# Nineteen filler products added in the first chunk, and three small sums moved from GpSimd to VectorE

## The chip, the cores and the metric

The kernel runs on one core of a Trainium2 chip. The core has five engines with a queue each: TensorE (PE in the profile, with its weight loads as PEld), VectorE (DVE), ScalarE (ACT), GpSimd (POOL) and SyncE (SP), which here only starts DMA transfers. An engine takes its instructions strictly in the order in which they were written into its queue, and waits on semaphores for what other engines must have done. The metric is the device time of one execution in microseconds, as the median of several runs.

## The reference

The input x has 2 sequences of 1024 steps and 128 channels. Four residual layers follow one another, each on a normalised x:

```python
x = x + attn_a(layernorm(x))   # projections, a scan with a decay per channel, norm, projection
x = x + ffn(layernorm(x))      # 8 experts: silu(x @ w_gate) * (x @ w_up) @ w_down, weighted
x = x + attn_b(layernorm(x))   # small MLPs, a recurrence with an 8x8 state per head, norm, MLP
x = x + ffn(layernorm(x))      # the same experts again
```

Each norm takes the mean and the variance of 128 channels and multiplies by 1/sqrt(variance + eps). The weights of the experts (the gate) are a product of two softmaxes over 8 logits.

## The kernel before

The 1024 steps of both sequences are cut into five chunks, four of 192 steps and one of 256, so that a chunk has 384 or 512 columns. Each chunk passes through the layers in pieces named by a letter and the chunk's number: A (attention a), f and F (gate and experts of the first ffn), B, P, R, C, O, E (attention b), g and G (second ffn). The pieces of different chunks are interleaved; the products of the experts are the bulk of TensorE's work, and the rest is put between them.

What is written is not the final order. Every operation is recorded as a step, and the method `order` (L488) plays the steps through a model of the five engines: it gives each step a rank, a cost and a due time, and at each point hands the engine that is free the ready step of the lowest rank. Tiles get their places (buffers) in the same pass, and a step that wants a place waits till one is free. `emit` (L690) then writes the steps in that order, all from line L703, which is why nearly every line of the profile reads L703 and is told apart by its tiles. A change of one step's engine changes the planner's due times, and so can reorder the steps round it.

The planner also sets *fillers*: products of a tile called turn with itself (128x128, in one pass), whose result nobody reads. Where its model sees TensorE idle for more than FILL = 350 ns ahead of a step (L657), it computes a number of fillers from the gap, and `emit` writes them ahead of that step (L700). They go into a bank of PSUM that is free, or into the bank of the step itself.

The start of the program, which the change touches, runs as follows for chunk 0:

- `part_a` (L1063): norm a0, its transpose pt_a0, three projections, the scan, then the output's transpose pt_ao0, norm aon0 and the update of x.
- `gating` (L1125) for f0: norm f0, three transposes into the tile pt_f0, then xT_hi (ScalarE) and xT_lo (VectorE), the logits pl_f0 (nine small products with wr), two softmaxes, and the transposes pc_f0 of the weights.
- `fold_small` (L926), independent of x: three products into the tile pf, which ScalarE copies into the tile fold (Z_at in the profile); VectorE fills in the rest of fold; then seven small products of fold with columns of vec into the tile pb (`m_at<-vec_at,Z_at`), from which VectorE makes the tile bias.
- `experts` (L1181) for f0. In this first use of each expert's weights, ScalarE and VectorE cut them into two parts (`wgu_at<-Z_at`) in a ring of six places; later chunks reload the cut weights. A part of an expert takes six products (`g_at<-xT_hi_at,wgu_at` and `xT_lo_at`), a Silu on ScalarE into the tile h, and a multiplication on VectorE. The products go into four banks named g; a bank comes free when its Silu or its multiplication has read it.

The norms are made by `layernorm` (L969). For a0, aon0 and f0, VectorE makes mean and variance (bn_stats, bn_aggr), and these two lines follow:

```python
either(f"ve_{name}", "P").tensor_scalar(ve[:, 0 : k.nt], mv[:, 0 : k.nt, 1], eps, None, ALU.add)
...
nc.gpsimd.tensor_tensor(rs[:, 0 : k.nt], ve[:, 0 : k.nt], expo.to_broadcast([P, k.nt]), ALU.pow)
```

`either` picks the usual engine ("P", GpSimd) unless the site's name stands in the set ENG (L110), in which case it picks the other.

## Time and profile before

| what | value |
|---|---|
| median of 3 runs | 766.05 us (765.82 to 766.85) |
| the profiled execution's own time | 766.12 us |
| its span, first to last instruction | 764.3 us |
| TensorE busy | 734.7 us (96%) |
| VectorE busy | 605.1 us (79%) |
| ScalarE busy | 457.7 us (60%) |
| GpSimd busy | 430.3 us (56%) |
| mean granted clock of TensorE | 0.99 |

The profiled execution lies 0.07 us above the median, and 1.82 us of its time lie outside its span. A busy TensorE in such a profile is one with products in flight, since the ends of products are modelled. The granted clock is the share of full speed that TensorE was given; before the first event of a trace the profile shows 1.00 for want of a record. Times in the text are microseconds from the span's start.

### The profile page before, as it was taken

Reading aid. Unit: us, or ns where it says so; the run is one execution under the profiler, and the core shown is the slowest. Engines: PE = TensorE matmul, PEld = TensorE weight load, DVE = VectorE, ACT = ScalarE, POOL = GpSimd, SP = SyncE. Lnnn points to the kernel's source line nnn. Section 1 sums busy time; section 2 is a strip of 40 time slices with the busy share of each in tenths; the row PEclk is TensorE's granted clock in tenths of the full one; section 3 lists DMA queues with packets and bytes.
Section 4 is the critical chain, followed back from the end, with each engine's and each line's share of the span. In section 5 each row is a group of like instructions: output and inputs, shape, how many; then the busy total and the mean of one; then the engine's idle time right before and its main releaser. Section 6 shows DMA issues by size and latency. Waiting matters only on the chain.

```text
span 764.3 us, 12089 instructions
## 1 busy us (share of the span) xinstructions
PE 734.7 (96%) x3406; PEld 575.2 (75%) x3406; DVE 605.1 (79%) x1387; ACT 457.7 (60%) x913; POOL 430.3 (56%) x491
## 2 busy tenths in 40 slices
PE   7899999999989999999998998999999999999997
PEld 7888787887777877766667767787787777776664
DVE  6576644699989998999999999999999778344332
ACT  3665577649774775644897969655654553554332
POOL 3132322977445597656975599975975247530222
PEclk9799999999999999999999999999999999999999
DMA  7597568666866589866495693686667857746551
GB/s 232 163 297 247 158 179 218 218 199 201 207 214 205 169 210 285 230 177 177 122 260 142 180 298 111 191 271 195 198 203 246 237 150 222 236 135 192 177 165 42
DMA packets 131561, 152.14 MB, mean 199 GB/s; under 512 B 52950, under 2 KB 74518, under 8 KB 131494
## 3 DMA queue, kind: packets, MB, share of 16 engines
q1 hardware_dynamic: 130694, 150.88, 67.2%
q8 instruction: 28, 0.46, 0.2%
q10 hardware_dynamic: 800, 0.48, 0.2%
q14 instruction: 39, 0.32, 0.1%
HBM read 131.79 MB, written 19.53 MB: 198 GB/s over the span
## 4 chain that ended last, share of the span: by engine, by line
PE 58%; DVE 17%; ACT 8%; POOL 6%; issue 5%; DMA 5%; SPq 0%; DVEq 0%; POOLq 0%; ACTq 0%
PE g_at L703 49%; PE m_at L703 8%; DVE h_at L703 3%; ACT L703 3%; DVE bu_at L703 2%; POOL ox_at L703 2%; ACT h_at L703 1%; DVE Z_at L703 1%; DVE pz_at L703 1%; DVE q_at L703 1%; DVE ot_at L703 1%; POOL pm_at L703 1%; DMA d_v<-b_at 1%; DVE y_at L703 1%; ACT Zt_at L703 1%
## 5 line engine op out<-in xcount | busy, mean ns | idle before, releaser
L703 PE MATMUL g_at<-xT_hi_at,wgu_at 128*128 128x384 f32 (+1 forms) x1280 | 481.1, 416 | 11.0 <-DVE h_at L703 4.3
L703 PEld LDWEIGHTS g_at<-xT_hi_at,wgu_at 128*128 128x128 f32 x1280 | 239.3, 190 | 76.0 <-issue 12.9
L703 ACT ACTIVATE h_at<-g_at 128x384 f32<-128x384 f32 (+1 forms) x320 | 162.6, 512 | 189.1 <-PE g_at L703 180.5
L703 PE MATMUL g_at<-h_at,wd_at 128*128 128x384 f32 (+1 forms) x640 | 267.2, 509 | 2.3 <-POOL h_at L703 0.9
L703 DVE TENSOR_TENSOR h_at<-h_at,g_at 128x384 f32<-128x384 f32 (+1 forms) x302 | 172.6, 575 | 100.7 <-PE g_at L703 55.4
L703 PE MATMUL g_at<-xT_lo_at,wgu_at 128*128 128x384 f32 (+1 forms) x640 | 226.3, 354 | 0.0
L703 PEld LDWEIGHTS g_at<-xT_lo_at,wgu_at 128*128 128x128 f32 x640 | 121.8, 190 | 38.8 <-issue 12.5
L703 PEld LDWEIGHTS g_at<-h_at,wd_at 128*128 128x128 f32 x640 | 116.2, 189 | 22.8 <-issue 3.1
L703 POOL TENSOR_TENSOR de_at<-de_at,cb_at 128x384 f32<-128x384 f32 (+1 forms) x50 | 54.2, 1085 | 94.9 <-ACT de_at L703 94.9
L703 ACT ACT_TABLE_LOAD x64 | 82.1, 1283 | 5.1 <-DMA x_at<-in_x 4.0
L703 POOL TENSOR_TENSOR ds_at<-ds_at,de_at 128x384 f32<-128x384 f32 (+1 forms) x58 | 66.4, 1145 | 24.4 <-DVE de_at L703 22.5
L703 POOL TENSOR_TENSOR Z_at<-Z_at,vr_at 128x192 f32<-128x192 f32 (+1 forms) x75 | 49.4, 659 | 33.2 <-DVE Z_at L703 30.1
L703 DVE TENSOR_TENSOR q_at<-bu_at,kt_at 128x384 f32<-128x384 f32 (+1 forms) x75 | 43.8, 583 | 0.7
L703 ACT COPY Zt_at<-Z_at 128x384 f32<-128x384 f32 (+1 forms) x40 | 39.2, 984 | 7.8 <-DVE Z_at L703 5.9
L703 DVE TENSOR_REDUCE bu_at<-pz_at 128x48 f32<-128x384 f32 (+1 forms) x75 | 43.3, 578 | 0.6
L703 POOL TENSOR_TENSOR ox_at<-Zt_at,y_at 128x384 f32<-128x384 f32 (+1 forms) x36 | 41.0, 1153 | 4.7 <-DVE y_at L703 4.6
L703 DVE TENSOR_TENSOR Z_at<-Z_at,q_at 128x384 f32<-128x384 f32 (+1 forms) x75 | 42.9, 572 | 0.8
L703 DVE TENSOR_TENSOR pz_at<-Z_at,bu_at 128x384 f32<-128x384 f32 (+1 forms) x75 | 42.8, 570 | 0.4
L703 ACT COPY de_at<-g_at 128x384 f32<-128x384 f32 (+1 forms) x50 | 24.9, 499 | 29.0 <-PE g_at L703 26.4
L703 POOL TENSOR_TENSOR vr_at<-vt_at,rks_at 128x384 f32<-128x384 f32 (+3 forms) x40 | 35.7, 895 | 1.1
L703 POOL TENSOR_TENSOR om_at<-Z_at,rst_at 128x384 f32<-128x384 f32 (+1 forms) x25 | 32.1, 1283 | 3.4 <-DVE Z_at L703 3.4
L703 POOL TENSOR_TENSOR h_at<-h_at,h_at 128x384 f32<-128x384 f32 x18 | 18.3, 1019 | 18.0 <-ACT h_at L703 18.0
(228 smaller groups left out, 1021.6 us busy)
## 6 DMA issues: line engine op xcount, KB each, us to landing
wgu_at<-wcut SPq DMA_DIRECT2D x288, 256.0 KB, 3.0
wd_at<-in_w_down SPq DMA_DIRECT2D x80, 256.0 KB, 2.9
wcut<-wgu_at SPq DMA_DIRECT2D x32, 256.0 KB, 4.4
cb_at<-cd_f SPq DMA_DIRECT2D x32, 192.0 KB, 3.7
cb_at<-cd_g SPq DMA_DIRECT2D x32, 192.0 KB, 3.4
Z_at<-in_w_gate SPq DMA_DIRECT2D x8, 256.0 KB, 3.5
Z_at<-in_w_up SPq DMA_DIRECT2D x8, 256.0 KB
cb_at<-cd_f SPq DMA_DIRECT2D x8, 256.0 KB
```

The costliest lines, as they stand in the source:

```text
L703: getattr(engine, s.call)(*[placed(v) for v in s.args], **{n: placed(v) for n, v in s.kw.items()})
```

## The change

A table MORE names two tiles, pb with 12 and pt_f0 with 7. Ahead of the first step on TensorE that writes into one of them, so many fillers are written, into that tile's own bank; the planner's computed fillers apply to all other steps. The three names ve_a0, ve_aon0 and ve_f0 are added to ENG, so that the sum of variance and eps of these three norms is made by VectorE; the power that follows stays on GpSimd.

```diff
+MORE = dict(pb=12, pt_f0=7)
 FILL_FROM, FILL_TO, FILL = 3300.0, 1e9, 350.0
...
-    ol3_3 ol3_7 ol4_1 ol4_3 ol4_7 ot0_2 ot1_2 ot2_2 ot3_2 rr1 v00 v01 v02 v03 v04 v21 vb1 vc1 ve_g4 vt1
-    xb2 ym0_0 ym1_0 ym2_0 ym3_0 ym4_0 ym4_2 ym4_3
+    ol3_3 ol3_7 ol4_1 ol4_3 ol4_7 ot0_2 ot1_2 ot2_2 ot3_2 rr1 v00 v01 v02 v03 v04 v21 vb1 vc1 ve_a0
+    ve_aon0 ve_f0 ve_g4 vt1 xb2 ym0_0 ym1_0 ym2_0 ym3_0 ym4_0 ym4_2 ym4_3
...
-                if e == "T" and t > free[e] + FILL and t < FILL_TO:
-                    to = s.args[0].tile
+                to = s.args[0].tile if e == "T" else None
+                if e == "T" and to.name in MORE and all(o is s or o.start is None for o in to.users):
+                    s.turns = (MORE[to.name], to.ring, to.place)
+                elif e == "T" and t > free[e] + FILL and t < FILL_TO:
```

The built programs differ in their order as follows. Up to the products into pf the queues of TensorE are the same, with 16 instead of 17 fillers ahead of pf. Then:

- before: 2 products into pb, 3 transposes pt_f0, 3 pb, 4 products of f0's first two parts with xT_hi, 1 pb, 9 logits, the 8 other products of these parts, 1 pb, 5 fillers, 3 transposes pc_f0, the third part's products.
- after: 7 fillers, 3 transposes pt_f0, 12 fillers, 2 pb, 2 products with xT_hi, 9 logits, the 10 other products, 3 pb, 3 transposes pc_f0, 2 pb, the third part's products. The 5 fillers ahead of pc_f0 are gone.

On VectorE, the copies into fold now follow the normalisation of f0, and the cut wb_lo stands inside the softmax, between its second and third operation. On ScalarE, the casts of wgu_f0_1_2 and wgu_f0_1_3 now stand between the softmax's exponentials and the load of the Silu table, ahead of the first Silu, h_f0_0_0; before, they stood behind the third and the fourth Silu. On SP's queue, the write-backs of these two cuts and the transfer of the gate weights (cd_f0) now stand ahead of the second half of the fourth expert's load. All of this lies at the start: the last step that has another place in the order is number 122 of 2811 on TensorE, 121 of 1387 on VectorE, 75 of 811 on ScalarE, 23 of 484 on GpSimd and 60 of 708 on SP. Behind these the queues are the same in both programs.

## The prediction

> **What bounds the kernel now.** I read the page first (busy shares, the slices with the clock, the chain), then the stretches of the first 45 us, then the instructions there.

> ```profile
> span 764.3 us, 12089 instructions
> PE 734.7 (96%) x3406; PEld 575.2 (75%) x3406; DVE 605.1 (79%) x1387; ACT 457.7 (60%) x913; POOL 430.3 (56%) x491
> PEclk9799999999999999999999999999999999999999
> PE 58%; DVE 17%; ACT 8%; POOL 6%; issue 5%; DMA 5%; SPq 0%; DVEq 0%; POOLq 0%; ACTq 0%
> ```

> TensorE is busy for 96% and carries 58% of the chain that ended last. Its clock is below full in one early slice, the second. All queues are the same in both programs behind TensorE's step 122 (the products pya_1, at about 43 us), so what the change is worth is how much earlier or later the engines stand there; TensorE is then busy without a gap (10.00 of 10 us in each stretch from 40 to 80 us), so that a lead or a lag is carried on.

> The next answer gives stretches that begin and end where the clock can step. Columns: stretch, its length, busy time (count) of PE, PEld, DVE, ACT and POOL, the granted clock, DMA share, GB/s.

> ```profile
> 14.57:17.98 3.41, 2.91 (x27) 2.77 (x26) 3.17 (x13) 0.83 (x4) 0.92 (x2) 1.00 0.93 293
> 17.98:21.39 3.41, 1.88 (x14) 1.53 (x13) 2.63 (x14) 0.95 (x2) 1.47 (x3) 1.00 0.40 113
> 21.39:24.81 3.42, 2.65 (x12) 2.60 (x13) 2.73 (x8) 1.94 (x9) 0.24 (x1) 0.50 1.00 321
> 24.81:28.22 3.41, 3.41 (x16) 3.41 (x15) 0.38 (x3) 1.14 (x6) 0.26 (x1) 0.50 0.87 308
> 28.22:31.63 3.41, 3.41 (x15) 3.41 (x13) 1.93 (x14) 2.87 (x6) 1.07 (x2) 0.50 0.02 7
> 407.10:410.51 3.41, 1.48 (x8) 1.01 (x6) 3.41 (x8) 2.29 (x4) 2.26 (x3) 1.00 0.15 38
> 451.47:454.88 3.41, 2.99 (x20) 2.42 (x18) 3.41 (x9) 2.58 (x4) 3.41 (x6) 1.00 0.97 329
> ```

> The clock steps at 21.39, 31.63, 410.51 and 413.93 us, all multiples of 3.41 us apart (10.24 is three of them). It fell to 0.50 after a stretch with PE busy 1.88 of 3.41 us, and after one with 1.48; it stayed full after 2.99. Between 1.88 and 2.99 the trace does not say. It rose after 28.22 to 31.63, full of long products, and not after 24.81 to 28.22, as busy but with nine 16-column products. So 10.24 us of the start run at half clock, and TensorE is busy for 9.47 of them.

> The instructions (start, duration, engine, line, operation, tiles, count, idle before and its releaser):

> ```profile
> 16.98 0.31 POOL L703 TENSOR_SCALAR ve_at<-mv_at 128x3 f32<-128x3 f32 x1 [6.89 <-DVE mv_at L703]
> 20.14 0.53 POOL L703 TENSOR_SCALAR ve_at<-mv_at 128x3 f32<-128x3 f32 x1 [1.86 <-DVE mv_at L703]
> 20.68 0.60 PE L703 MATMUL m_at<-vec_at,Z_at 128*128 128x1 f32 x4 [1.43 <-DVE bias_at L703]
> 22.16 0.90 PE L703 MATMUL m_at<-cst_at,xn_at 128*128 128x128 f32 x3 [0.87 <-DVE xn_at L703]
> 28.64 1.28 ACT L703 ACT_TABLE_LOAD   x1
> 29.93 0.87 ACT L703 ACTIVATE h_at<-g_at 128x384 f32<-128x384 f32 x2
> 32.21 0.47 ACT L703 COPY xT_at<-m_at 8x384 f32<-8x384 f32 x1 [1.03 <-PE m_at L703]
> 33.73 0.39 ACT L703 CAST wgu_at<-Z_at 128x256 fp32r<-128x256 f32 x1
> 34.41 0.47 ACT L703 CAST xs_hi_at<-m_at 128x384 fp32r<-128x384 f32 x1
> ```

> Two of the three sums, then TensorE's gaps of 1.43 and 0.87 us, then ScalarE's order: table, Silus at 29.93, and only later the casts.

> **The three sums.** On GpSimd, from the end of the statistics to the start of the power: 4.23 to 4.64, 16.90 to 17.37, 20.05 to 20.75, that is 0.41, 0.47 and 0.70 us. On VectorE the nearest row is ve of norm a1: starts 28.17, takes 0.16, and the power starts at 28.41, 0.24 after it; with 0.03 us between dependent VectorE rows (sn ends at 29.16, dn starts at 29.19) it is 0.27. Gains 0.14, 0.20 and 0.43. Of the first, half is kept: TensorE runs 8.85 to 11.15 at half pace (products 0.32 us apart, then 0.17), and if that step up stays at its place, work brought forward by 0.14 is worth 0.07. On VectorE the sums add 3 x 0.16 us where it has idle time or work that waits for them anyway (the cuts of wgu behind them are needed at 24 us). Sum: f0's transposes at 22.16 - 0.07 - 0.20 - 0.43 = **21.46 us**. Bounds: -0.5 to -0.8.

> **The fillers, and where they stand.** Warm, 17 fillers took 2.09 us, so 0.11 each; cold, 5 took 1.24, so 0.21 each. Twelve and seven warm are 1.36 and 0.79 us, nearly the gaps of before (1.43 ahead of pb, 0.87 ahead of pt_f0). But the order has turned: pt_f0 now comes first. The seven run right behind pf, from about 19.0 to 19.8, and TensorE then stands idle till 21.46. The twelve run behind the transposes, where TensorE's next work was 1.2 us off at most.

> Does the clock hold? In 17.98 to 21.39, PE would be busy with the last filler (0.14), pf (0.93), seven fillers (0.79 plus a tail of 0.17): 2.0 us, against 1.88 that did not hold it and 2.99 that did. Nearest row: it falls. I take that. What follows, at half clock, each step from the rows of before:

> - transposes 21.46 to 22.15 (0.69 to the next issue, as 22.16 to 22.85);
> - twelve fillers x 0.21 = 2.52, to 24.67. ScalarE's xT_hi is ready at 22.85 (it starts 0.93 after the transposes, takes 0.48), so some 1.8 us of this is pure delay;
> - two pb products, 4 rows x 0.19 (six took 22.85 to 23.99) = 0.76, to 25.43;
> - two products with xT_hi x 0.355 (four took 23.99 to 25.41) = 0.71, to 26.14;
> - nine logits x 0.213 (25.70 to 27.62) = 1.92, to 28.06 (before: 27.62);
> - ten products x 0.32 (28.08, 28.40, ...) = 3.20, last ends at 31.45 (before, eight: 30.52).

> **The casts ahead of the first Silu.** The cast of wgu_f0_1_3 needs the second of the six wgu places, which the last of these ten products frees. Ahead of it ScalarE is done by about 30.3. So: cast from 31.50, 0.40; table 1.28 with its issue; first Silu at 33.2 against 29.93. ScalarE then copies the gate (xT_at) at 33.63 against 32.21, +1.42, and casts xs_hi, with one cast less between, at 33.2 + 3.07 = 36.27 against 34.41, +1.86. TensorE's third part needs the bank that the first Silu frees: 33.7 against 31.93, +1.77. ScalarE is busy 8.56 of 10 us from 30 to 40, all of it from 34 to 38, so it can't make this good. Behind this nothing differs but the lag. I take **+1.8 us**, between +1.4 (ScalarE's lag at the gate) and +2.2.

> **Costed at nothing, with their cover.** wb_lo inside the softmax (1.09 us): gate ready at about 31.0, while TensorE reaches pc_f0 at 32; without that cover, up to +0.7. The five fillers that go (1.24 cold): they stood where TensorE waited for the gate. SP: the fourth expert's second half waits for the last pb, about 33 against 30.77; its first cast was at 43.91, so 10 us of cover; without it +2. The write-backs ahead of it are waits of the same length. GpSimd loses three rows of 0.25 to 0.53.

> **Sum** against the profiled execution's own time: 766.12 + 1.8 = **767.9 us** (0.07 above the median of the runs, which is left as it is).

> [...]

> **Rivals.**

> 1. *The clock holds.* If 2.0 of 3.41 us is enough, or the boundary lies such that the idle 1.6 us is shared by two stretches. For: the range 1.88 to 2.99 is open, and fillers are denser work than the pb rows they replace (128 columns against 1). Against: nearest row. Then: transposes 0.55 to 22.0, fillers 1.36 to 23.4, pb 4 x 0.15 to 24.0, xT_hi 2 x 0.17 to 24.35, logits 9 x 0.11 (rows at 86.87 to 87.90) to 25.35, ten x 0.17 to 27.1; casts to 27.9, table to 29.2, first Silu 29.2; third part at 29.7 against 31.93, -2.2, xs_hi 32.27 against 34.41, -2.1. Time 766.1 - 2.1 = **764.0**. It decides once the fall is avoided for the whole 10 us; each 3.41 us of it gives back about 1.3.
> 2. *The lag is partly regained.* If the clock's step up falls later than 31.63 in an execution, before loses up to half of 2.5 us of long products, while after waits for its Silu then anyway: +1.8 - 1.2 = +0.6. Or the lag ends in one of the later waits (TensorE is idle 1.59 us between 130 and 140 us). Time 766.1 to 767.5, say **766.8**.
> 3. *The cold stretch grows by one step*, because the idle time ahead of 33.7 and the logits leave 28.22 to 31.63 too light: 2.5 us of products at half pace more, +1.2: **769.1**.

> That the change does not do what it says is partly the forecast itself: the fillers are written, but one group lies after the gap for which its number fits.

> **How the numbers follow.** Runs of this kernel lie within 0.14% of each other, so 0.2% (1.53 us) is about what can be told from no change. Chances: forecast 0.42, rival 1 0.31, rival 2 0.21, rival 3 0.06. Slower by over 0.2% (above 767.6): 0.9 of the forecast and rival 3, 0.44; faster (below 764.5): 0.9 of rival 1, 0.28; the rest, 0.28, within. The likeliest one's own range is 767.4 to 768.5; the whole reaches from rival 1's time to rival 3's, 763.8 to 769.1.

> **What would show it.** In the profile after: the first transposes of f0 at 21.4 to 21.5 (sums right); a clock of 0.50 from about 21.4 to 31.6 (fillers don't hold it) or 1.00 throughout (rival 1); the twelve fillers behind the transposes, about 2.5 us long; first Silu at 33.2, with the table's load behind two casts and a ScalarE wait for g_at ahead of the second; the products of the third part at 33.7; then the same lag at, say, 43 and 100 us (if it shrinks there, rival 2). The prediction is wrong if the clock holds, or if the second cast does not wait for TensorE.

## The result, and the profile after

| | median | range |
|---|---|---|
| changed kernel | 770.32 us | 764.64 to 777.37 |
| kernel before, beside it | 766.95 us | 764.84 to 775.36 |
| ratio | 1.0036 | 95% interval 1.0020 to 1.0051 |

The changed kernel is slower, by 0.36% (2.8 us). The forecast had the sign right and the size wrong: 767.9 us was forecast, and the median lies above the end of the range (769.1). Single executions of both kernels spread over 10 to 13 us; the three runs of before that the prediction had to go by had spread over 1.03. Ratios and mean clocks in this text leave out executions more than 1.5% above the fastest of their kernel, and a ratio is not the quotient of the two medians beside it (here 1.0044); where they differ, the text goes by the ratio.

The page of the profiled execution of the changed kernel (its own time 771.37 us), with the lines that answer to those shown of before:

```profile
span 769.6 us, 12118 instructions
PE 739.2 (96%) x3419; PEld 577.5 (75%) x3419; DVE 605.3 (79%) x1390; ACT 457.8 (59%) x913; POOL 430.8 (56%) x488
PEclk9699999999999999999999999999999999999999
PE 52%; DVE 23%; ACT 8%; issue 7%; DMA 5%; POOL 4%; SPq 0%; ACTq 0%; DVEq 0%; POOLq 0%
```

TensorE is busy for 96% of the span, as before. Its clock dips lower in the second slice, 6 tenths in place of 7. The clock steps in this trace at 20.58, 30.82, 34.24, 37.65, 655.46 and 658.88 us, all multiples of 3.41 us apart, as in before; the stretches between such points show why. The columns are those of the same view of before: length, busy time of PE, PEld, DVE, ACT and POOL, granted clock, DMA share, GB/s.

```profile
17.17:20.58 3.41, 2.54 (x20) 2.16 (x19) 2.84 (x14) 1.14 (x3) 1.36 (x2) 1.00 0.64 205
20.58:24.00 3.42, 2.76 (x13) 2.61 (x14) 2.14 (x9) 1.73 (x8) 0.24 (x2) 0.50 0.58 179
24.00:27.41 3.41, 3.41 (x17) 3.41 (x17) 0.00 (x0) 0.85 (x3) 0.23 (x1) 0.50 1.02 367
27.41:30.82 3.41, 3.41 (x12) 3.41 (x13) 2.64 (x12) 1.40 (x7) 0.13 (x1) 0.50 0.06 22
30.82:34.24 3.42, 2.37 (x19) 2.12 (x19) 1.82 (x11) 2.97 (x6) 1.26 (x2) 1.00 0.58 178
34.24:37.65 3.41, 3.41 (x13) 3.14 (x13) 1.67 (x5) 2.45 (x7) 1.00 (x1) 0.50 0.89 277
652.05:655.46 3.41, 1.39 (x9) 0.94 (x7) 3.41 (x4) 0.62 (x2) 1.04 (x2) 1.00 0.71 252
```

The first fall and its 10.24 us are as before (20.58 to 30.82). Then comes one that before does not have: after the stretch 30.82 to 34.24 the clock falls a second time. What lies in that stretch, on TensorE and on ScalarE (start, duration, engine, line, operation, tiles, count, idle before and its releaser):

```profile
18.71 1.00 PE L703 MATMUL m_at<-turn_at 128*128 128x128 f32 x7
21.24 0.99 PE L706 MATMUL m_at<-cst_at,xn_at 128*128 128x128 f32 x3 [1.53 <-DVE xn_at L706]
21.88 2.80 PE L703 MATMUL m_at<-turn_at 128*128 128x128 f32 x12
31.04 0.72 PE L706 MATMUL m_at<-vec_at,Z_at 128*128 128x1 f32 x6
31.63 0.49 PE L706 MATMUL m_at<-cst_at,cw_at 128*8 128x128 f32 x3
31.95 0.50 PE L706 MATMUL m_at<-vec_at,Z_at 128*128 128x1 f32 x4
33.50 0.44 PE L706 MATMUL g_at<-xT_hi_at,wgu_at 128*128 128x384 f32 x1 [1.05 <-ACT h_at L706]
```

```profile
31.24 0.41 ACT L706 CAST wgu_at<-Z_at 128x256 fp32r<-128x256 f32 x1 [1.31 <-PE g_at L706]
31.66 1.28 ACT L706 ACT_TABLE_LOAD   x1
32.96 0.49 ACT L706 ACTIVATE h_at<-g_at 128x384 f32<-128x384 f32 x1
```

From 31.04 to 33.50 TensorE has only one-column products, three small transposes and a wait of 1.05 us for the first Silu, which itself stands behind a cast that waited 1.31 us for TensorE and behind the table.

The lag against before is read at the same product in both traces, here one of the down-projections, first of before and then of the changed kernel:

```profile
50.46 0.81 PE L703 MATMUL g_at<-h_at,wd_at 128*128 128x384 f32 x2
```
```profile
53.76 0.81 PE L706 MATMUL g_at<-h_at,wd_at 128*128 128x384 f32 x2
```

53.76 - 50.46 = +3.30 us. It was +1.57 at the third part's products, 33.50 above against this row of before:

```profile
31.93 0.42 PE L703 MATMUL g_at<-xT_hi_at,wgu_at 128*128 128x384 f32 x1
```

So the second fall made 1.73 of it. It is +3.0 at 100 us, +1.7 at 230 to 290, +0.9 at 300, +3.1 to +3.8 at 350 to 390, +2.8 at 430 to 590 and +5.25 from 660 us on, behind a third fall (after 652.05 to 655.46).

### The profile page after: what moved, and what is told of

The parts are those of the page before. It is cut to its first block, busy times and chain, and to the rows that moved or that the text cites. A ratio compares the mean times of both kernels' runs of the same rounds, so it can differ in the third digit from the quotient of the medians.

```text
span 769.6 us, 12118 instructions
## 1 busy us (share of the span) xinstructions
PE 739.2 (96%) x3419; PEld 577.5 (75%) x3419; DVE 605.3 (79%) x1390; ACT 457.8 (59%) x913; POOL 430.8 (56%) x488
## 4 chain that ended last, share of the span: by engine, by line
PE 52%; DVE 23%; ACT 8%; issue 7%; DMA 5%; POOL 4%; SPq 0%; ACTq 0%; DVEq 0%; POOLq 0%
PE g_at L706 45%; PE m_at L706 7%; DVE h_at L706 4%; ACT L706 3%; DVE bu_at L706 2%; DVE Z_at L706 2%; DVE pz_at L706 2%; DVE q_at L706 2%; ACT h_at L706 2%; DVE ot_at L706 1%; DMA pm_at<-zd 1%; DMA d_v<-b_at 1%; DVE cm_at L706 1%; ACT b_at L706 1%; POOL pm_at L706 1%
## 5 line engine op out<-in xcount | busy, mean ns | idle before, releaser
L706 ACT COPY de_at<-g_at 128x384 f32<-128x384 f32 (+1 forms) x50 | 25.0, 500 | 29.0 <-PE g_at L706 27.5
L706 POOL TENSOR_TENSOR rs_at<-ve_at,expo_at 128x3 f32<-128x3 f32 (+1 forms) x25 | 23.0, 930 | 20.2 <-DVE ve_at L706 19.2
```

What stands on the lines that cost most here:

```text
L706: getattr(engine, s.call)(*[placed(v) for v in s.args], **{n: placed(v) for n, v in s.kw.items()})
```

## The experiments

In each, the medians are set against the kernel before on the same chip; "start lag" is the difference worked out as above, between 45 and 80 us, against the one trace of before. It comes from one execution each, the medians from several.

### One part of the change at a time

The fillers alone, the sums alone in the order that the planner then makes, the sums moved without a new order, and both without a new order:

```diff
 # fillers alone: ENG as before, and
+MORE = dict(pb=12, pt_f0=7)
 # sums alone: the changed kernel with
-MORE = dict(pb=12, pt_f0=7)
+MORE = dict()
 # sums in place: the order planned as before, and in emit
+on = "V" if s.call == "tensor_scalar" and s.args[0].tile.name in IN_PLACE else s.engine
 # both in place: the line above and MORE of the change
```

> The nineteen fillers alone; the three sums stay on GpSimd, and the order of before stays (pb, then pt_f0). Theory 'order' (the fillers are fitted to the gaps of before; the moved sums turned the order, so that seven stand ahead of a gap too long for them and twelve behind it, and two casts stand ahead of the first Silu): here the twelve fill the gap of 1.43 us and the seven that of 0.87, TensorE is busy for over 3 of the 3.41 us there, the clock stays at 1.00 from about 11 us on, the first Silu comes at 27.5 instead of 29.9, and the time is 764.5 against 767.0 of before. Rival 'fillers cost' (nineteen products in the way, wherever they stand): first Silu later than 29.9, time 768 to 769. Rival 'phase' (the two kernels differ only by where the clock happens to fall later on): same spread and median as before, 767.

> The three sums alone, in the order that the planner then makes (the one of the changed kernel, casts ahead of the first Silu); the twelve fillers ahead of pb are gone, and the planner by itself puts eight ahead of pt_f0 where the change put seven. Theory 'order': transposes at 21.3, the clock falls, the logits start 2.5 us earlier than in the changed kernel, first Silu about 30.7 (before 29.9, changed 33.0), time 767.8, so that most of the loss goes with the twelve fillers. Rival 'sums' (the move of the sums and its order carry the loss): first Silu near 33, time 770. Rival 'phase': 767 to 770 with the spread of both.

> The three sums on VectorE at the place that they have in the order of before; nothing else moves, no added fillers. Theory 'order': f0's transposes at 21.4 to 21.5 instead of 22.16, the clock falls as before, first Silu 29.3, time 766.4. Rival 'sums': slower than before, 769 to 770. Rival 'phase': not to be told from before.

> Both parts in the order of before: the sums on VectorE in place, twelve fillers ahead of pb and seven ahead of pt_f0 in their gaps. Theory 'order': the clock holds through 20 to 32 us, first Silu 27.0 to 27.5, time 764.4, better than before by 2.5. Rival 'fillers cost': 768. Rival 'sums': 769 or more. Rival 'phase': 767.

| kernel | median (before) | ratio, 95% interval | start lag |
|---|---|---|---|
| fillers alone | 767.90 (767.72) | 1.0000, 0.9980 to 1.0021 | +0.3 |
| sums alone, new order | 770.16 (767.72) | 1.0015, 0.9988 to 1.0042 | +0.5 |
| sums in place | 766.11 (767.72) | 0.9975, 0.9956 to 0.9994 | +0.3 |
| both in place | 767.01 (767.72) | 0.9994, 0.9968 to 1.0019 | +1.2 |

The three sums are a gain (0.25%) when nothing else moves. Where it comes from is not shown: in the trace of that kernel f0's transposes begin at 22.20, not at the 21.4 to 21.5 expected (22.16 in before), with the first rise of the clock 0.55 us later. The nineteen fillers, placed in the gaps for which their numbers fit, change the time by nothing that these runs can tell (0.2% either way). The sums in the planner's new order are not told from the kernel before, nor from the changed kernel.

The fillers alone were expected to hold the clock, and in the trace they did not. These are its stretches, columns as before; the clock fell at 21.67:

```profile
14.85:18.26 3.41, 2.90 (x27) 2.79 (x26) 3.15 (x12) 0.93 (x5) 1.05 (x2) 1.00 0.89 301
18.26:21.67 3.41, 3.41 (x29) 3.13 (x28) 2.51 (x13) 1.08 (x2) 1.47 (x3) 1.00 0.37 87
```

TensorE is busy for the whole of the second stretch, 3.41 of 3.41 us, and the clock still falls. So busy time, by which the prediction had read it, did not hold it here.

### Longer fillers

Three kernels with fillers of 384 columns. In the first, sums in place, eight stand ahead of pb and three ahead of pt_f0, in the order of before; in the second, the changed kernel's order, thirteen ahead of pt_f0 alone; in the third, as the first, the planner's own fillers are long too.

```diff
-MORE = dict(pb=12, pt_f0=7)
+MORE = dict(pb=8, pt_f0=3)          # second kernel: dict(pt_f0=13)
...
+to = bank[:, 0 : 3 * P].rearrange("p (a d) -> p a d", a=3)
+zs = z.unsqueeze(1).to_broadcast([P, 3, P])
-matmul(bank[:, 0:P], z, z, start=True, stop=True)
+matmul(to, z, zs, start=True, stop=True)
...
-n = int(((t - first) * 0.8 - 100) / (110 if free[e] else 215))   # third kernel only
+n = int(((t - first) * 0.8 - 100) / (170 if free[e] else 320))
```

> The order of before with the three sums on VectorE, and fillers of 384 columns in place of those of 128: eight ahead of the first product into pb and three ahead of the first transpose of f0. A warm 384-column product is issued every 0.17 us, a 128-column filler every 0.11, so the long ones carry twice the columns in the same time. Theory 'columns': what holds the clock is the columns that stream, not the busy time, since with 128-column fillers the clock fell at 21.67 after a stretch in which TensorE was busy 3.41 of 3.41 us. Then the first fall comes 3.4 us later or not at all in most executions, the mean granted clock of the runs is 0.993 or more in at least half of them, and the median is 764 to 765.5. Rival 'threshold higher' (the 64-row and one-column products in that stretch keep it too light whatever the fillers are): the fall stays near 21 to 23 us, the fillers run cold, and the median is 766.5 to 768, as with 128-column fillers in the same order (767.0).

> The changed kernel's order and sums, with thirteen fillers of 384 columns ahead of the first transpose of f0 (2.2 us warm, in the gap of 2.3 us that seven fillers of 128 columns fill for 0.8) and none ahead of pb. Theory 'columns': the clock falls a step later or not at all in most executions, nothing cold stands behind the transposes, first Silu at 29.5 to 31, median 765.5 to 767.5. Rival 'casts alone': the clock falls at the same place or later, but the casts still wait for the tenth product and the Silu for them, so that the stretch before 34 us is light and falls again; the median is 768.5 to 770.5 as in the changed kernel.

> The run with long fillers in place (sums on VectorE, eight and three fillers of 384 columns, order of before), and the planner's own fillers too are of 384 columns, their number worked out with 170 and 320 ns for one in place of 110 and 215. Theory 'columns': stretches at 4 to 8, 450 and 650 us get more columns, the first rise comes one step of 3.41 us earlier in some executions and later falls are rarer; throttled time falls below the 7.9 us mean of the run with long fillers in two places only, median 763 to 765. Rival: the lead is taken up by waits for ScalarE and VectorE behind 300 us; the clock is higher and the median stays at 765 to 766.

> The kernel with long fillers throughout once more, to tell its gain from no change: the ratio's interval was 0.9937 to 0.9998. Expected 0.995 to 0.998, the clock full from 10 us on in most executions. If the gain was chance, the ratio is 0.999 or more.

| kernel | median (before) | ratio, 95% interval | start lag |
|---|---|---|---|
| long fillers, order of before | 765.54 (768.04) | 0.9968, 0.9948 to 0.9988 | -3.6 |
| long fillers, changed order | 768.30 (768.04) | 1.0000, 0.9977 to 1.0024 | +0.2 |
| all fillers long | 764.21 (768.05) | 0.9968, 0.9937 to 0.9998 | -3.8 |
| all fillers long, again | 762.70 (769.75) | 0.9919, 0.9888 to 0.9949 | -3.8 |

The same gaps, filled for about the same time, now hold the clock at the start: it is 1.00 from 17.88 to 28.12 us. Stretches of the first kernel, and its fillers:

```profile
17.88:21.29 3.41, 3.36 (x24) 2.95 (x22) 2.99 (x15) 1.04 (x3) 1.17 (x2) 1.00 0.40 111
21.29:24.70 3.41, 3.41 (x24) 2.92 (x23) 2.64 (x8) 2.38 (x10) 0.36 (x2) 1.00 0.77 233
```
```profile
19.24 1.69 PE L710 MATMUL m_at<-turn_at 128*128 128x384 f32 x8
```

Busy time is the same as in the kernel that fell (3.36 against 3.41); the columns are not. If each product is counted with the columns that it streams, in the stretch in which it starts, the fallen stretch of the fillers alone has 2948, the first one here 4484. Counted so over the twenty traces of this case, between 10 and 755 us, the stretches of 3.41 us at full clock fall into these three groups:

| columns in the stretch | stretches | clock fell after it |
|---|---|---|
| under 2304 | 30 | 28 |
| 2304 to 3072 | 71 | 15 |
| over 3072 | 4186 | 0 |

A stretch filled with 384-column products, one each 0.174 us in before (its median from 40 to 80 us), would have some 7,500, an estimate (3.41 / 0.174 x 384). The 128-column filler takes 0.11 us for 128 columns (the 17 from 16.30 us on in before), 1,160 a us, and the 384-column product 2,200. The second stretch above, with 2780, lies in the middle band and held, where the one with 2948 fell: within that band the count does not tell (15 falls after 71 stretches). In the changed order the thirteen long fillers kept the clock one step longer in the trace (first fall at 24.43, behind a stretch with 1684 columns, among them the logits), and the second fall came as in the changed kernel (27.84 to 31.26 has 2318 columns, as 30.82 to 34.24 there).

The mean time at half clock of the runs, (1 - mean clock) x 2 x span, is 7.9 us with the long fillers against 16.5 beside it, and 14.7 with the nineteen short ones in the same order. So the clock is the long fillers' doing. The time gained is 2.5 us, not half of 8.6, and the three sums alone had gained 1.9: the intervals do not tell how much of it the fillers make. In the trace the lead is -3.6 us at 80 us, -4.3 at 290, about 0 at 390 us of before, -3.0 again from 420 to 590, and -0.6 at the end, behind a fall of the clock at 649.35 that before does not have. The costliest groups of TensorE between 320 and 350 us of this kernel (busy, mean ns, idle before):

```profile
L711 PE MATMUL g_at<-xT_hi_at,wgu_at 128*128 128x512 f32 x51 | 23.9, 504 | 1.6 <-DVE h_at L711 1.6
```

The same work in before (323 to 353 us):

```profile
L703 PE MATMUL g_at<-xT_hi_at,wgu_at 128*128 128x512 f32 x54 | 24.8, 497 | 0.0
```

TensorE waits there for VectorE's multiplications, and in before it does not. But that is no price of coming early. The slowest kernel below, changed with pb early, comes there 5.4 us late and waits as long (326 to 360 us):

```profile
L713 PE MATMUL g_at<-xT_hi_at,wgu_at 128*128 128x512 f32 x58 | 26.7, 497 | 1.7 <-DVE h_at L713 1.7
```

Before has its idle time later, 2.2 us between 400 and 415 against 0.9 here, and its clock falls there (410.51). So this wait says as much of the one trace of before as of the lead.

The kernel with all fillers long is faster than the kernel before in both measurements, and in the second, where the changed kernel stood beside it (769.40), than that too. Only the second interval lies wholly below that of the sums in place. Its page's line of the clock the second time:

```profile
PEclk9999999999999999999999999999999999999999
```

### The casts ahead of the first Silu

The cause that the prediction named. First the cure: in the changed kernel, and in the one with the sums alone, the casts of wgu_f0_1_2 and 1_3, their cuts and write-backs go behind the multiplication of the second part (h_f0_0_1).

```diff
+for s in steps:
+    if name(s) not in BACK: out.append(s)
+    if s.engine == "V" and name(s) == "h_f0_0_1": out += held   # wgu_f0_1_2, wgu_f0_1_3, wcut_1_2, wcut_1_3
```

> The changed kernel, but the casts of wgu_f0_1_2 and wgu_f0_1_3, the cuts VectorE makes of them and their write-backs stand behind the first multiplication of the experts, so behind the first Silu, as before; fillers, sums and the rest of the new order stay. Theory 'casts': the wait of the second cast for the tenth product is what costs. Then the first Silu starts at 30.0 to 30.6 us (32.96 in the changed kernel), the third part's products at 31.9 to 32.4 (33.50), no second fall of the clock comes at 34, the lag at 45 to 80 us is +0.5 to +1.2 (changed kernel +3.3), and the median is 0 to 1 us above the kernel before, in place of 3. Rival 'late steps': the kernels differ by the cold steps they meet much later (400 to 660 us), the start alone moves nothing that lasts; then the start looks as above, and the median still lies 2 to 3 us above the kernel before.

> As the run with the casts put back, but without the nineteen fillers (the planner then puts 8 of its own ahead of the transposes of f0 and none ahead of pb). Theory 'casts': with neither the twelve cold fillers nor the wait, the first Silu starts at 28.5 to 29.5, the third part at 31.0 to 31.8, the lag at 45 to 80 us is -0.5 to 0, and the median lies 0.5 to 1.5 us below the kernel before, near the run with the sums moved in place (ratio 0.9975). Rival 'new order as such': whatever the casts do, the other moves (transposes first, wb_lo inside the softmax, the write-backs ahead on SP) cost; then the median is as with the sums alone in the new order, 2 to 3 us above the kernel before.

In these two kernels, and only in them, two parts of the second expert's weights are cut from a buffer that the fourth expert's load has by then overwritten (it is issued at 25.24 us in the trace of the first, and the casts begin at 34.89; in the changed kernel 32.50, behind the casts), so the share of that expert in the output differs. The instructions are the same in number and size, and the trace shows no wait ahead of the casts.

With the fillers it came to 771.99 against 768.04 us (1.0051, 1.0024 to 1.0077), start lag +5.5; without them to 769.14 (1.0018, 0.9995 to 1.0042), start lag +0.3. The first Silu began early (31.52, with this execution's whole start 1.1 us later than that of the changed kernel), and yet the clock stayed at half from 23.43 to 40.50 us. Both expectations missed: putting the casts back does not cure the changed kernel, and without the fillers it does not make the order faster than before.

Then the cause by itself, in the kernel before, with no filler and no sum touched:

```diff
+at = max(i for i, s in enumerate(rest) if name(s) == "pu_f0_0_1") + 1
+return rest[:at] + casts + first + rest[at:]     # casts, cuts, write-backs, and then the first Silu
```

> The kernel before with one move alone: the casts of wgu_f0_1_2 and wgu_f0_1_3 (with their cuts and write-backs) stand ahead of the first Silu, behind the last of the eight products of the first two parts; no filler and no sum is touched. Theory 'casts': the Silu waits for the last product (30.52 in the kernel before), two casts of 0.4 and the table's 1.28, so it starts at about 32.3 in place of 29.93 and the third part's products come at 32.8 to 33.2 in place of 31.93; median +0.8 to +2.5 us. Rival 'not the casts': they cost only the start, which later waits take back, or they are not what made the changed kernel slower; median within 0.7 us of the kernel before.

770.61 against 768.05 us, ratio 1.0031 (1.0007 to 1.0054). ScalarE in its trace, the second cast, the table and the first two Silus:

```profile
30.93 0.41 ACT L713 CAST wgu_at<-Z_at 128x256 fp32r<-128x256 f32 x1 [0.88 <-PE g_at L713]
31.36 1.28 ACT L713 ACT_TABLE_LOAD   x1
32.65 0.87 ACT L713 ACTIVATE h_at<-g_at 128x384 f32<-128x384 f32 x2
```

The Silu starts at 32.65 (29.93 in before, 32.3 expected), the start lag is +1.4, and the time is longer by about what the whole change costs. So the early casts, with the Silu behind them, are enough to make the kernel slower, though taking them out of the changed kernel is not enough to make it well.

### Fillers, casts and the products into pb

The changed kernel with ScalarE's order at the first Silus as before (the casts behind the second Silu, ahead of the loads that overwrite their source); the same without the nineteen fillers (eight of the planner's own then stand ahead of pt_f0, as in the sums alone); and the changed kernel and the sums alone once more:

```diff
+return (rest[:silu] + on("S", second) + on("S", casts) + rest[silu:mult]
+        + on("V", second) + on("V", casts) + on("D", casts) + rest[mult:])
-MORE = dict(pb=12, pt_f0=7)     # the second kernel only
+MORE = dict()
```

> The changed kernel, with ScalarE's order at the first Silu as before: table, the first two Silus one behind the other, then the casts of wgu_f0_1_2 and wgu_f0_1_3, then the copy of the gate (the loads that overwrite their source come behind them). Fillers, sums and all other moves stay. In the run with the casts put back alone, the second Silu still stood behind the copy of the gate and began at 34.1. Theory 'order on ScalarE': with both Silus early, no TensorE wait at the third part, the second fall goes, and the median is 0 to 1.2 us above the kernel before (the twelve cold fillers alone). Rival 'cold fillers': the products stay 1.8 us late and meet the same falls; the median stays 2 to 3.5 us above.

> The run with the two Silus first and the casts behind them, now also without the nineteen fillers: the sums on VectorE and the rest of the new order are left (transposes first, wb_lo inside the softmax, the write-backs where they stood). Theory 'two costs': fillers and casts each delay the start, and with neither the start is no later than before; third part's products at 30.8 to 32.0 us, lag at 45 to 80 us -1.0 to +0.4, median between 1.5 us below and 0.7 us above the kernel before. Rival 'new order as such': the lag is +1 or more, or the median lies 1.2 to 2.5 us above, as with either cost alone.

> The changed kernel once more, beside the others. Theory 'two costs': lag at 45 to 80 us of +2.5 to +3.5, as in its first trace (+3.3) and near the sum of the fillers alone (+1.9) and the casts alone (+1.4); median 2 to 3.5 us above. If the second fall was an accident of that one execution, the lag is +1.5 to +2.2, as forecast, and the clock falls once at the start.

> The sums alone in the planner's new order, once more: early casts, no twelve fillers. Theory 'two costs': lag +0.5 to +1.5 and a median 1 to 2.5 us above the kernel before (first time: 770.16 against 767.72), less than the changed kernel. Rival 'fillers are nothing': as slow as the changed kernel, 2.5 us or more above.

| kernel | median (before) | ratio, 95% interval | start lag | at half clock at the start |
|---|---|---|---|---|
| Silus first | 770.76 (768.05) | 1.0024, 0.9994 to 1.0055 | +1.9 | 10.2 us |
| neither fillers nor early casts | 770.54 (769.75) | 1.0002, 0.9967 to 1.0036 | +3.3 | 17.1 us |
| changed kernel again | 769.40 (769.75) | 1.0007, 0.9972 to 1.0041 | +3.8 | 10.2 + 3.4 us |
| sums alone again | 770.95 (769.75) | 1.0014, 0.9983 to 1.0044 | +1.9 | 6.8 + 3.4 us |

The second trace of the changed kernel has the second fall again (after 31.54 to 34.95), and so has that of the sums alone: it was no accident of one execution. These times are too wide to tell the four apart, and the second measurement of the changed kernel alone does not tell it from before. Nor is the kernel with the Silus first cured, though its trace has no second fall: over its executions the mean time at half clock is 19.2 us, against 21.0, 19.0 and 18.7 for the others and 16.3 to 16.8 for before beside them. But the kernel with neither is as late at the start as the changed one, so that "two costs that add up" did not cover it. Its stretches:

```profile
24.76:28.17 3.41, 3.41 (x14) 3.41 (x14) 1.80 (x7) 2.10 (x10) 0.14 (x1) 0.50 1.01 359
28.17:31.59 3.42, 3.42 (x17) 3.25 (x16) 0.63 (x5) 2.65 (x6) 1.07 (x2) 0.50 0.04 14
31.59:35.00 3.41, 3.35 (x12) 2.75 (x12) 2.83 (x12) 2.33 (x6) 1.00 (x1) 0.50 0.01 2
35.00:38.41 3.41, 3.41 (x11) 2.63 (x10) 2.25 (x6) 2.21 (x11) 0.00 (x0) 0.50 0.86 281
```

Always busy, and at half clock for five steps. In 28.17 to 31.59, where before has its eight long products and rises, this order has part of the ten, then five products into pb and the three transposes pc_f0. Also VectorE's bias operations wait for those products, ahead of the first multiplication:

```profile
32.11 0.16 DVE L721 TENSOR_TENSOR bias_at<-m_at,b_at 128x3 f32<-128x3 f32 x1 [3.21 <-PE m_at L721]
```

That pointed at a third thing in the new order: five of the seven products into pb stand behind the ten products, where before had six ahead of the logits and one behind its eight. Two kernels test it, one with neither fillers nor early casts, and the changed kernel with this move alone:

```diff
+pb = [s for s in steps if s.engine == "T" and s.args[0].tile.name == "pb"]
+at = steps.index(pb[0])
+rest = [s for s in steps if s not in pb]
+return rest[:at] + pb + rest[at:]
```

> The run with neither fillers nor early casts, and all seven products into pb stand together behind the transposes of f0, ahead of the logits (in that run five of them stood behind the ten long products). Theory 'light products': the stretch behind the logits then holds the ten long products, three transposes and the third part, the clock rises at the third step as in the kernel before (10.24 us at half clock), the multiplication of the first part does not wait for the bias (32.69 in the run with neither), the lag at 45 to 80 us is -1.0 to +0.5, and the median lies 0 to 2 us below the kernel before. Rival: the cold stretch is still 13.7 us or longer, or a second fall comes; lag +1 or more, median no better than before.

> The changed kernel with that move alone: all seven products into pb behind the twelve fillers, casts and fillers as they are. If the light products are the whole cause of the second fall, it goes, the lag at 45 to 80 us is +1.4 to +2.2 and the median 0.5 to 2 us above the kernel before. If the casts' wait (1.3 us) and the table load behind it are enough, the stretch before the third part is still light, the clock falls again near 34 us, and lag (+3 to +4) and median stay as in the changed kernel.

| kernel | median (before) | ratio, 95% interval | start lag | at half clock at the start |
|---|---|---|---|---|
| neither, pb early | 767.00 (768.15) | 0.9979, 0.9950 to 1.0008 | +0.6 | 10.2 us |
| changed, pb early | 773.43 (768.15) | 1.0069, 1.0043 to 1.0094 | +7.6 | 20.5 us |

With the casts and pb put back and the nineteen fillers gone, what is left of the new order is not slower than before, though its interval overlaps that of the same kernel with pb late. With pb early but fillers and casts as changed it is the slowest of all, with a lag that neither theory had (+1.4 to +2.2, or +3 to +4): the products into pb then lie, cold and behind the twelve cold fillers, ahead of the ten products for whose last the cast waits, and TensorE waits longer still:

```profile
34.06 0.84 PE L713 MATMUL m_at<-cst_at,cw_at 128*8 128x128 f32 x3
36.56 0.69 PE L713 MATMUL g_at<-xT_hi_at,wgu_at 128*128 128x384 f32 x1 [1.66 <-ACT h_at L713]
```

The two kernels of this pair differ in the fillers (the change's nineteen against eight of the planner's) and in the place of the casts and the second Silu, and by 6.4 us.

### A pure delay

The prediction carried a lag at 40 us to the end unchanged. In the kernel before, 24 fillers of 128 columns were put where TensorE has no gap:

```diff
+MORE = dict(pg_f0_4_0=24)
```

> The kernel before, with 24 fillers of 128 columns ahead of the first product of pg_f0_4_0 (near 53 us), where TensorE has no gap and runs at full clock: a pure delay of 24 x 0.11 = 2.6 us, and nothing else. It measures what the prediction assumed, that a lag is carried on unchanged. Theory 'carried': median +2.3 to +2.9 us. Rival 'partly taken back' (the lead of 3.6 us of the run with long fillers had shrunk to 0.6 at the end, with waits for the Silus at 320 to 350 us): median +0.5 to +1.6 us.

769.56 against 768.05 us, ratio 1.0033 (1.0004 to 1.0062). In the trace the lag steps by 2.68 us at the place (from -0.36 to +2.32), is +0.8 at 300 us, +3.5 at 360 to 390, +0.5 at 440 to 470, and then +2.7 to +3.3 to the end. The interval, 0.3 to 4.8 us, holds both theories. That a delay at the start costs time is shown; how much of it lasts is open in this kernel. All nineteen traces set against that of before say more: the lag at the end rises by 0.82 us for each us of lag behind the start (correlation 0.79), with a scatter of 1.9 us. Most of a lag is carried, and single executions differ by more than is lost.

## Why the prediction was wrong

**The three sums: the sign right, the size not shown.** The forecast had 0.70 us for them at f0's transposes, 21.46, within 0.5 to 0.8; they began at 21.24, 0.92 earlier than in before, but with the first rise of the clock 0.8 us earlier too. Moved alone they gain 0.25%, 0.06 to 0.44, that is 0.5 to 3.4 us, and the trace of that run has the transposes no earlier.

**Fillers, clock, casts, Silu, third part: right to 0.3 us.** The seven fillers ran at 18.71, TensorE then idled for 1.53 us, the clock fell, the twelve fillers ran cold behind the transposes (the forecast has 2.52 us for them, from the first issue to the next work; 21.88 to 24.48 is 2.60). First Silu 32.96 (forecast 33.2), third part 33.50 (33.7). The early casts, which the forecast named as the cause, are shown to cost by themselves (1.0031).

**"Behind this nothing differs but the lag. I take +1.8 us": wrong.** At the third part the lag was +1.57. The step that failed is the next one, which the sum put at nothing: after the stretch in which TensorE waits for the late Silu (30.82 to 34.24, 2.37 us busy, 2318 columns) the clock falls a second time, which is 1.73 us, and the lag is +3.3 in one trace and +3.8 in the other. The executions agree: those of the changed kernel are at half clock for 19.3 us on the mean (19.0 when run again), those of before in the later runs for 15.4 to 16.8. That this alone makes the distance from 767.9 to 770.32 is not shown; the second measurement, 1.0007 (0.9972 to 1.0041), would hold the forecast's +1.8 us as well. This is close to the third rival, which had a chance of 0.06 and a price of 1.2 us. It was underrated because the prediction looked for a cold stretch that ends later, and did not hold the stretch behind its end, 31 to 34 us, against the rows of the clock, though it had TensorE's wait and the small products there in its own sum. TensorE is busy for 2.37 us of it, inside the bracket of 1.88 to 2.99 that the prediction itself had left open.

**PE's busy time as the measure of the clock: wrong.** The bracket "1.88 that did not hold it and 2.99 that did" gave the right answer for the first stretch by luck: that one, 17.17 to 20.58, was busy for 2.54 us, not the 2.0 reckoned with, and its 2176 columns put it with the 30 under 2304, of which 28 fell. But after 3.41 of 3.41 us busy, with 128-column fillers, the clock fell, and in twenty traces it fell after none of the 4186 stretches with over 3072 columns. By the columns, 30.82 to 34.24 (2318) is one that may well fall: of the eleven with 2304 to 2432 (both included), seven did.

**"A lead or a lag is carried on": on average, not in one execution.** With a lag of +3.3 to +3.8 at 45 to 80 us, the two traces of the changed kernel end at +5.25 and -0.14. Till 290 us it shrinks by 1.2 to 1.6 us in both, but so does the +0.3 of the fillers alone (to -1.3), so that is no sign of a lag being made good. A fall of the clock elsewhere moves the lag too: by 1.6 us at the one in the first trace of the changed kernel, 650 to 660 us (+3.6 to +5.2), and by 1.1 the other way at the one in before's trace, 408 to 415 (+3.8 to +2.7). Large lags and leads last: +7.6 us ends as +7.3, +5.5 as +5.4, and of the two runs of the kernel with all fillers long, -3.8 ends as -1.8 and -3.6.

**"Runs of this kernel lie within 0.14% of each other": wrong.** Three runs were too few. The place of the 3.41 us steps against the program differs between executions: the first rise comes at 11.15 us in before, 10.34 and 11.06 in the two traces of the changed kernel, 13.37 in the sums alone, and the falls are whole steps from there (10.24 us, three of them, in before and in both traces of the changed kernel). The forecast gave a single value where single executions of one kernel spread over 10 to 13 us.

**What the cause is, as far as it is shown.** The new order has three things that can make the start longer: twelve fillers that run cold in front of the logits, the casts in front of the Silu's table, and four more one-column products behind the long ones, in a stretch after which the clock fell (34.24 in the changed kernel) or did not rise (31.59 with neither fillers nor early casts). For the third there is the trace alone, and in the changed kernel itself undoing it made things worse (1.0069). Early casts alone cost 0.31% (0.07 to 0.54). Fillers and casts together (and the second Silu's place) make 0.9% between the last pair, with pb early in both. Taking all three out gives 0.9979 (0.9950 to 1.0008). Open is the share of the fillers alone (1.0024, 0.9994 to 1.0055) and of the late pb alone (1.0002, 0.9967 to 1.0036, with a start 3.3 us late in its one trace).

## What to carry to other kernels

## What the runs showed that was not expected

- TensorE lost its clock after a stretch in which it was busy for 3.41 of 3.41 us (21.67, fillers alone). In the twenty traces, after stretches of 3.41 us with under 2304 columns it fell 28 times in 30, after the 4186 with over 3072 not once. At half clock it rose after none of 33 stretches with under 2432 columns, after 17 of 21 with 2432 to 3201, and after all 25 above.
- The spread of this kernel, 764 to 775 us without its slowest execution, goes with the cold steps: a straight line through the changed kernel's executions rises by 0.56 us for each us at half clock (correlation 0.75; 0.52 and 0.68 in those of before), which is 1.9 us for a step of 3.41.
- The kernels differ by it too: over the eighteen runs, each against before beside it, the ratio follows the mean time at half clock with a correlation of 0.85, and 0.42 us of time go with each us of it. The kernel with all fillers long, 10 to 13 us less at half clock, is 0.3 to 0.8% ahead.
